# Last layer's adapter of a Trainium2 kernel: masked over all eight adapters, or gathered for each sequence onto strips of the array

## The chip, the cores and the metric

The kernel runs on one core of one Trainium2 chip. The metric is the device time of one execution in microseconds. A trace of one execution, taken by the hardware profiler, comes with it: it lists the instructions of TensorE (PE, with its weight loads as PEld), VectorE (DVE), ScalarE (ACT), GpSimd (POOL) and SyncE (SP), the DMA transfers, and the waits between them.

## The reference

Four layers are added in turn to x, which holds 64 sequences of 64 tokens with 512 features, in fp32. The first multiplies each sequence by a matrix chosen for it, the second is a linear layer with a low-rank adapter, the third attends over a paged cache in a window of 256 positions. The fourth is the one that is changed:

```python
# x: (64, 64, 512); W: (512, 512); A: (8, 16, 512); Bm: (8, 512, 16); adapter_idx: (64,)
H = jnp.einsum('btd,od->bto', x, W)
A_b = A[adapter_idx]
B_b = Bm[adapter_idx]
s_b = scalings[adapter_idx]
xa = jnp.einsum('btd,brd->btr', x, A_b)
delta = jnp.einsum('btr,bor->bto', xa, B_b)
x = x + H + delta * s_b[:, None, None]
```

In the third layer a sequence has eight query heads, four key heads and a block table; the keys and values that its window can reach are gathered by index. The index of the adapter lies in 0 to 6, one for each of the 64 sequences.

## The kernel before

There are two stages. The first (until about 450 us of the trace) goes through 32 tiles of 128 tokens, two sequences each: it runs the first two layers, the queries, keys and values of the third, the writing of new cache rows, and all index arithmetic. Its order is written out by hand in a loop over n, and small pieces of setup are hung onto single values of n. One of these is `adapters` (L425 to L441): for the last layer it builds `mask3`, with a row for each of the 128 pairs of adapter and rank and a column for each sequence; an entry is the adapter's scaling where the sequence uses that adapter, and otherwise zero. Another is `late_inputs` (L388): its last part loads the adapter's two matrices, `a3_sb` and `bm_sb`, whole.

The second stage goes through 16 groups q of four sequences. A group has eight steps, one for each sequence b and each pair of key heads gp; the step within a group is i, from 0 to 7. A step s does, in this order on TensorE:

- `scores(s + 1)` (psc, L975): the two key heads of the next step, each on 64 rows of the array;
- `turn_p(s)` (pp, L1017): six transposes of this step's softmax weights;
- in steps 4 to 7 a `k_turn` (psk, L175): four transposes of the next group's keys;
- one entry of the list `parts`, described below;
- `values(s)` (po, L1033): weights times values, each of two key heads on 64 columns of the array;
- in steps 3 to 6 another `k_turn`.

VectorE and ScalarE do the softmax of step s + 1 meanwhile (`maxima`, `exponentials`, `shares`), copy the transposed weights (pT, L1024) and the transposed keys (`kT_mem`, L183 and L184), and ScalarE and VectorE make the window's penalty `pen` (L963 to L965) in every second step. po needs both copies pT of its step.

GpSimd issues the gathers of the cache, all in the helper at L65, in program order: `v_load` (four for each sequence, into `vs_mem`, three sequences ahead), `v_patch` (one, into `vt_mem`, after ScalarE's `v_copy` at L197), and for each group `k_patch` in step 1 and `k_load` in steps 2 and 3, for keys of a later group. `v_share` (L208) then moves 28 rows of the values inside SBUF over SyncE's queue. In group 0, and only there, TensorE, VectorE and GpSimd also finish the last queries (`product_q`, L258; `norm_q`, where GpSimd has L232, L233 and L244; `turn_q`, L272).

`parts` is filled at the end of a group by `last_parts(q)` and worked off in the eight steps of the next, one entry in each. Entries 0 to 3 are `out_product` (pso, L1051): the attention's output product for 128 features, added to `xq` by VectorE (L1054). Entries 4 to 7 are the last layer: in step 4 the ranks (psxa, L1059) of all eight adapters for 256 tokens, their product with the mask on VectorE (xa, L1062), and half of the base product of the first 128 tokens (psy, L1070); in step 5 its other half (L1076), the product of the masked ranks with `bm_sb` (L1078), ScalarE's copy `ys` (L1081) and the store; in steps 6 and 7 the same for the other 128 tokens. `residual3` (L672) has added the identity to the transposed W beforehand, so that psy holds the residual too. After group 15 the list of eight parts runs alone, one after another.

PSUM tiles pso, psxa and psy come from one pool of two banks, `psM`.

Of the kernel before, what the change touches and what calls it, by code (L numbers as in the profile page):

```python
# [10 lines left out]
F32 = mybir.dt.float32  # L11
I32 = mybir.dt.int32
# [38 lines left out]
def kernel(  # L51
# [58 lines left out]
    w3_sb = ctile([P, KC, D], F32, "w3_sb")  # L110
    a3_sb = ctile([P, KC, P], F32, "a3_sb")
    bm_sb = ctile([P, D], F32, "bm_sb")
    iod = ctile([P, 3, 4, 28], F32, "iod")
    ion = ctile([P, 3, 4, 28], F32, "ion")
    mask3 = ctile([P, B], F32, "mask3")
    cen = ctile([P, B], F32, "cen")
# [166 lines left out]
    with ExitStack() as one:  # L283
# [104 lines left out]
        def late_inputs(part):  # L388
            h = slice(part % 2 * 2, part % 2 * 2 + 2)
            if part < 2:  # L390
                S.dma_start(out=woT_sb[:, h], in_=woT[:, h])
            elif part < 4:
                S.dma_start(out=w3_sb[:, h], in_=w3T.rearrange("(c p) o -> p c o", p=P)[:, h])
            else:
                S.dma_start(out=a3_sb, in_=a3T.rearrange("(c p) r -> p c r", p=P))
                S.dma_start(out=bm_sb, in_=bm3)

# [14 lines left out]
        def rows0():  # L412
# [9 lines left out]
            for h, hs in halves():  # L422
                V.tensor_scalar(
                    cidx[hs], condf[hs].rearrange("p (n two) -> p n two", two=2)[:, :, h],
                    float(T), tcol[hs], ALU.mult, ALU.add)  # L425

        def adapters(ad_i, scb, e, dst):
# [442 lines left out]
        for n in range(NLAST):  # L870
# [40 lines left out]
            if n % 4 == 3:  # L911
                mixers(n // 4 + 2)
            if 5 <= n < 10:
                late_inputs(n - 5)
            if 14 <= n < 18:
                positions(n - 14)
            if n == 19:
                adapters(ad3_i, sc3b, 8, mask3)
                middles()
# [123 lines left out]
    def last_parts(q):  # L1043
# [12 lines left out]
        def ranks():  # L1056
            ps = bank(psM, f"psxa{q}")
            for c in range(KC):
                PE.matmul(ps[:, :256], lhsT=a3_sb[:, c, :], rhs=xq[:, c],  # L1059
                          start=(c == 0), stop=(c == KC - 1))  # L1060
            xa[0] = mp.tile([P, 4, T], F32, name=f"xa{q}", tag="xa")
            V.tensor_tensor(  # L1062
                xa[0], ps[:, :256].rearrange("p (b t) -> p b t", t=T),
                mask3[:, 4 * q : 4 * q + 4].unsqueeze(2).to_broadcast([P, 4, T]), ALU.mult)

        def y_first(i):
            n = 2 * q + i
            psy[i] = bank(psM, f"psy{n}")
            for c in range(2):
                PE.matmul(psy[i], lhsT=xq[:, c, i * P : (i + 1) * P], rhs=w3_sb[:, c, :],  # L1070
                          start=(c == 0), stop=False)

        def y_rest(i):
            n = 2 * q + i
            for c in range(2, KC):
                PE.matmul(psy[i], lhsT=xq[:, c, i * P : (i + 1) * P], rhs=w3_sb[:, c, :],  # L1076
                          start=False, stop=False)
            PE.matmul(psy[i], lhsT=xa[0].rearrange("p b t -> p (b t)")[:, i * P : (i + 1) * P],  # L1078
                      rhs=bm_sb, start=False, stop=True)
            ys = ap2.tile([P, D], F32, name=f"ys{n}", tag="ys")  # L1080
            S.copy(ys, psy[i])  # L1081
            S.dma_start(out=out[n * P : (n + 1) * P, :], in_=ys)

        return [lambda ec=ec: out_product(ec) for ec in range(KC)] + [
            lambda: (ranks(), y_first(0)), lambda: y_rest(0), lambda: y_first(1), lambda: y_rest(1)]

# [22 lines left out]
    for s, (q, b, gp) in enumerate(steps):  # L1109
# [13 lines left out]
        if i in (2, 3):  # L1123
            k_load(q + 2, i - 2)
        scores(s + 1)
        turn_p(s)
# [82 lines left out]
```

## Time and profile before

| | |
|---|---|
| time, median of 3 runs (lowest, highest) | 1235.95 us (1233.83, 1238.47) |
| profiled execution: its own time | 1233.95 us |
| profiled execution: span of the trace | 1232.2 us |
| mean granted TensorE clock | 0.976 |
| second stage, from the first po to the end | 491.3 to 1232.2 us |
| one group, po to po eight steps later, groups 2 to 14 | mean 44.6 us |
| psxa in a group: 8 records, start to start | 1.76 us |
| one gather of `vs_mem` on GpSimd, mean | 1206 ns |

A row of the trace that begins with L names the line of the kernel, the engine, the operation, the tile that is written and, after the arrow, what is read; then the shape and the count; in brackets the idle time of the engine before it and what ended it. A matmul of fp32 operands appears as two records. A matmul's recorded duration includes its way through the array, so consecutive records overlap, and a rate is read from the distance of their starts. For TensorE a shape such as 124*64 gives the rows and columns of the array that are used.

### The profile page before, as it was taken

What the parts mean: (1) busy time and instruction counts of PE and PEld (TensorE: products, weight loads), DVE (VectorE), ACT (ScalarE), POOL (GpSimd) and SP (SyncE); (2) the same over time, 40 slices, a digit from 0 to 9 for tenths busy, and PEclk for the clock granted to TensorE, in tenths of its full rate; (3) what the DMA queues carried; (4) which work ended last, traced back from release to release, by engine and by line L of the source; (5) the groups of instructions that cost most, each with busy time, mean ns of one, the idle gap of its engine ahead of it and who ended that gap; (6) DMA issues with size and microseconds to landing.
All of it is one profiled execution on the core that took longest, in us unless ns stands there. A gap on an engine that the chain in (4) does not pass through costs nothing.

```text
span 1232.2 us, 17756 instructions
## 1 busy us (share of the span) xinstructions
PE 1112.6 (90%) x5622; PEld 642.5 (52%) x5622; DVE 750.7 (61%) x2312; ACT 568.2 (46%) x1471; POOL 613.4 (50%) x603
## 2 busy tenths in 40 slices
PE   4999899999999968788998998899999999999998
PEld 4444434444444434455655665555665565655565
DVE  3785347767656656784665664665665665666561
ACT  1332222233222435454665664665665665566651
POOL 3243322332335346776556655656666665665520
PEclk9999999999999988898999998999999999999999
DMA  8375613223342493636455645645745654665420
GB/s 265 126 265 212 227 39 112 96 78 106 98 141 67 148 182 96 162 88 151 130 133 132 157 116 112 149 119 133 167 127 131 152 142 110 154 145 132 98 63 35
DMA packets 129820, 163.20 MB, mean 132 GB/s; under 512 B 58079, under 2 KB 96891, under 8 KB 125545
## 3 DMA queue, kind: packets, MB, share of 16 engines
q0 software_dynamic: 63872, 85.04, 28.9%
q1 hardware_dynamic: 55632, 62.28, 16.8%
q10 hardware_dynamic: 10224, 14.76, 3.5%
q8 instruction: 45, 0.74, 0.3%
q14 instruction: 47, 0.39, 0.1%
HBM read 139.66 MB, written 50.33 MB: 154 GB/s over the span
## 4 chain that ended last, share of the span: by engine, by line
PE 73%; DVE 8%; DMA 6%; issue 5%; POOL 4%; ACT 3%; another core or an unknown queue 0%; ACTq 0%; SPq 0%; POOLq 0%; DVEq 0%
PE pso L1051 8%; PE pp L1017 8%; PE ps L776 7%; PE po L1033 7%; PE kv L809 7%; PE psc L975 7%; PE q L258 5%; PE psy L1076 5%; PE psy L1070 4%; PE psk L175 4%; PE psxa L1059 2%; PE ps L778 2%; PE psy L1078 2%; PE ps L752 2%; POOL vs_mem L65 2%
## 5 line engine op out<-in xcount | busy, mean ns | idle before, releaser
L65 POOL DMA_INDIRECT vs_mem<-in_vblk_dram,iv_old x256 | 308.9, 1206 | 78.1 <-issue 72.2
L65 POOL DMA_INDIRECT vt_mem<-pv,iv_new x64 | 81.1, 1266 | 177.3 <-ACT vt_mem L197 99.1
L1001 ACT ACTIVATE sm_mem<-sm_mem,mn 128x336 f32<-128x336 f32 x256 | 145.6, 574 | 38.1 <-DVE mn L991 31.9
L991 DVE CUSTOM_DVE_ANT_0 sm_mem<-psc,pen 128x336 f32<-128x336 f32 x256 | 119.8, 500 | 49.9 <-PE pp L1017 23.0
L1033 PE MATMUL po<-pT,vt_mem 124*64 124x128 f32 x1536 | 118.8, 282 | 14.4 <-issue 7.5
L1033 PEld LDWEIGHTS po<-pT,vt_mem 124*64 124x64 f32 x1536 | 84.7, 136 | 89.7 <-ACT sm_mem L1001 45.6
L258 PE MATMUL q<-wq_sb,x2q 128*128 128x512 f32 x256 | 120.0, 614 | 6.9 <-DMA x2q<-x2d 6.9
L1017 PE MATMUL pp<-ident,sm_mem 128*124 128x128 f32 x768 | 117.5, 287 | 7.5 <-DVE rsum L1008 3.3
L1051 PE MATMUL pso<-oT,woT_sb 128*128 128x256 f32 x512 | 122.3, 383 | 0.8 <-ACT oT L1041 0.8
L1017 PEld LDWEIGHTS pp<-ident,sm_mem 128*124 128x124 f32 x768 | 82.9, 141 | 73.0 <-issue 63.2
L975 PE MATMUL psc<-kT_mem,qs 64*128 64x336 f32 x512 | 110.0, 507 | 10.7 <-DVE kT_mem L184 10.1
L809 PE MATMUL kv<-wkv_sb,xr 128*128 128x512 f32 x256 | 117.1, 602 | 1.1 <-DVE k L224 1.1
L776 PE MATMUL ps<-kT_mem,kT_mem 128*128 128x512 f32 x256 | 117.0, 600 | 0.6 <-PE ps_fill L482 0.6
L1009 DVE TENSOR_SCALAR sm_mem<-sm_mem,rsum 128x336 f32<-128x336 f32 x256 | 105.3, 411 | 9.1
L1051 PEld LDWEIGHTS pso<-oT,woT_sb 128*128 128x128 f32 x512 | 91.8, 191 | 13.5 <-ACT pen L965 1.9
L244 POOL TENSOR_TENSOR q<-q,rsq 128x512 f32<-128x512 f32 x30 | 32.2, 1073 | 128.9 <-DVE rsq L242 82.4
L175 PE MATMUL psk<-ident,k 84*128 84x84 f32 x512 | 64.9, 254 | 34.8 <-ACT kT_mem L184 9.1
L258 PEld LDWEIGHTS q<-wq_sb,x2q 128*128 128x128 f32 x256 | 49.8, 199 | 65.7 <-issue 56.3
L1024 DVE COPY pT<-pp 124x384 f32<-124x384 f32 x128 | 70.8, 553 | 21.6 <-PE pp L1017 7.9
L776 PEld LDWEIGHTS ps<-kT_mem,kT_mem 128*128 128x128 f32 x256 | 49.0, 192 | 61.6 <-issue 60.7
L809 PEld LDWEIGHTS kv<-wkv_sb,xr 128*128 128x128 f32 x256 | 47.5, 193 | 58.4 <-issue 55.6
L1024 ACT COPY pT<-pp 124x384 f32<-124x384 f32 x128 | 61.8, 482 | 33.5 <-PE pp L1017 30.1
(223 smaller groups left out, 1750.4 us busy)
## 6 DMA issues: line engine op xcount, KB each, us to landing
xt<-in_x_dram SPq DMA_DIRECT2D x32, 256.0 KB
x2d<-xr SPq DMA_DIRECT2D x8, 1024.0 KB
x2q<-x2d SPq DMA_DIRECT2D x32, 256.0 KB
qd<-qt SPq DMA_DIRECT2D x64, 128.0 KB
qs<-qd SPq DMA_DIRECT2D x16, 512.0 KB
xq<-x2d SPq DMA_DIRECT2D x16, 512.0 KB
out_dram<-ys ACTq DMA_DIRECT2D x32, 256.0 KB
vt_mem<-vt_mem SPq DMA_DIRECT2D x192, 28.0 KB
```

The lines of the kernel that those rows point to most:

```text
L65: G.indirect_dma_start(out=dst, out_offset=None, in_=src, in_offset=bass.IndirectOffsetOnAxis(ap=idx, axis=0), **more,)
L175: PE.transpose(ps[:, oq, :], k2[:NP, 4 * oq + o4, 2 * gp : 2 * gp + 2].rearrange("p g d -> p (g d)"), ident[:NP, :NP])
L258: PE.matmul(psq[n], lhsT=xt[:, c, :], rhs=wq_sb[:, c, :], start=(c == 0), stop=(c == KC - 1))
L776: PE.matmul(ps, lhsT=wb_sb[:, c, oc * P : (oc + 1) * P], rhs=x1_mem[:, c, :], start=(c == 0), stop=False)
L809: PE.matmul(pskv[n], lhsT=xrs[s][:, c, i * P : (i + 1) * P], rhs=wkv_sb[:, c, :], start=(c == 0), stop=(c == KC - 1))
L975: PE.matmul(pscs[s][g], lhsT=qts[q][gs, gp, b % 4].rearrange("p h t -> p (h t)"), rhs=kT(q, gp)[gs, b % 4].rearrange("p o c i -> p (o c i) ...
L991: V.tensor_tensor_reduce(rows4(sm)[:, :, :, :28], rows4(pscs[s][g]), rows4(pens[b]), SCALE, 3.0e38, ALU.add, ALU.min, mn)
L1001: S.activation(w, w, AF.Exp, bias=mn, scale=-1.0, accum_out=rsum)
L1017: PE.transpose(pp[:NVK, o, :], sms[s][g][0][:, o * P : o * P + NVK], ident)
L1024: (V.tensor_copy if g else S.copy)(pT, pps[s][g][:NVK])
L1033: PE.matmul(po[g * HD : (g + 1) * HD, :], lhsT=vt(b)[:NVK, o, 2 * gp + g], rhs=pTs[s][g][:, o, :], start=(o == 0), stop=(o == 2))
L1051: PE.matmul(o, lhsT=woT_sb[:, c, ec * P : (ec + 1) * P], rhs=oT[:, c // 2, :, c % 2, :], start=(c == 0), stop=(c == 3))
```

## The change

The last layer's adapter is no longer held for all eight adapters. For each group the weights of its four sequences are gathered by GpSimd: four gathers (`a_load`) of 128 rows of 256 bytes into `a3_mem`, one for each sequence, and one gather (`b_load`) of 128 rows of 2 KB into `b3_mem`. They are issued in steps 5, 6 and 7 of the group whose tokens they are for; the products that read them run in steps 4 and 5 of the next group.

The ranks of one tile of 128 tokens (two sequences, 16 ranks each) take 32 columns of the array. There are four strips of 32 columns: token tile i (0 or 1) and feature chunk c modulo 2 choose the strip, and chunks c and c + 2 add up in it. `b3_mem` holds the output rows twice for each token tile, so the product with the ranks also sums the two strips; that product takes 64 rows of the array for each token tile. The mask remains, now to keep, of the two sequences on a strip, the one that the token belongs to, with its scaling.

The base product's chunks are divided otherwise over the steps: in step 4 the first chunk of the first tile, in step 5 the first chunk of the second tile and both products with the ranks, in steps 6 and 7 three chunks and the store of one tile each.

In the first stage, `last_adapters` takes the place of the second call of `adapters`, at the same place in the order; it makes the two index lists `ia3` and `ib3` and the new mask. The fifth part of `late_inputs` goes.

```diff
-    a3_sb = ctile([P, KC, P], F32, "a3_sb")
-    bm_sb = ctile([P, D], F32, "bm_sb")
+    a3_mem = ctile([P, 4, 16, KC], F32, "a3_mem")
+    b3_mem = ctile([P, D], F32, "b3_mem")
-    mask3 = ctile([P, B], F32, "mask3")
+    mask3 = ctile([P, B // 4, 2], F32, "mask3")
+    ia3 = ctile([P, B], I32, "ia3")
+    ib3 = ctile([P, B // 4], I32, "ib3")
...
-            else:
-                S.dma_start(out=a3_sb, in_=a3T.rearrange("(c p) r -> p c r", p=P))
-                S.dma_start(out=bm_sb, in_=bm3)
...
+        def last_adapters():
+            adf = t1([P, B], F32, "adf8")
+            V.tensor_copy(adf, ad3_i)
+            V.tensor_scalar(ia3, adf, float(P), pcol, ALU.mult, ALU.add)
+            seq_i, r_i = t1([P, 1], I32, "seq_i"), t1([P, 1], I32, "r_i")
+            own_s, r_f = t1([P, 2], F32, "own_s"), t1([P, 1], F32, "r_f")
+            V.tensor_copy(seq_i, pcol)
+            V.tensor_scalar(r_i, seq_i, 15, None, ALU.bitwise_and)
+            V.tensor_copy(r_f, r_i)
+            V.tensor_scalar(seq_i, seq_i, 4, 1, ALU.arith_shift_right, ALU.bitwise_and)
+            V.tensor_copy(own_s[:, 1:], seq_i)
+            V.tensor_scalar(own_s[:, :1], own_s[:, 1:], -1.0, 1.0, ALU.mult, ALU.add)
+            scl, part = t1([P, B], F32, "scl8"), t1([P, B], F32, "part8")
+            V.tensor_scalar(scl, adf, 0.0, sc3b[:, :1], ALU.is_equal, ALU.mult)
+            for e in range(1, 8):
+                V.tensor_scalar(part, adf, float(e), sc3b[:, e : e + 1], ALU.is_equal, ALU.mult)
+                V.tensor_tensor(scl, scl, part, ALU.add)
+            pick = part[:, : B // 2].rearrange("p (q s) -> p q s", s=2)
+            for h, hs in halves():
+                own_b = own_s[hs].unsqueeze(1).to_broadcast([HD, B // 4, 2])
+                two = slice(2 * h, 2 * h + 2)
+                V.tensor_tensor(mask3[hs], scl[hs].rearrange("p (q i) -> p q i", i=4)[:, :, two],
+                                own_b, ALU.mult)
+                V.tensor_tensor(pick[hs], adf[hs].rearrange("p (q i) -> p q i", i=4)[:, :, two],
+                                own_b, ALU.mult)
+            idx = scl[:, : B // 4]
+            V.tensor_reduce(idx, pick, AX.X, ALU.add)
+            V.tensor_scalar(ib3, idx, 16.0, r_f, ALU.mult, ALU.add)
...
             if n == 19:
-                adapters(ad3_i, sc3b, 8, mask3)
+                last_adapters()
                 middles()
...
         def ranks():
-            ps = bank(psM, f"psxa{q}")
+            ps = bank(psM, f"psxa{q}")[:, :P]
             for c in range(KC):
-                PE.matmul(ps[:, :256], lhsT=a3_sb[:, c, :], rhs=xq[:, c],
-                          start=(c == 0), stop=(c == KC - 1))
+                for i in range(2):
+                    lo = i * 64 + c % 2 * 32
+                    PE.matmul(ps[lo : lo + 32, :],
+                              lhsT=a3_mem[:, 2 * i : 2 * i + 2, :, c].rearrange("p b r -> p (b r)"),
+                              rhs=xq[:, c, i * P : (i + 1) * P], start=(c < 2), stop=(c >= 2))
...
-        def y_first(i):
+        def y_base(i, cs, start=False, stop=False):
             n = 2 * q + i
-            psy[i] = bank(psM, f"psy{n}")
-            for c in range(2):
+            if start:
+                psy[i] = bank(psM, f"psy{n}")
+            for c in cs:
                 PE.matmul(psy[i], lhsT=xq[:, c, i * P : (i + 1) * P], rhs=w3_sb[:, c, :],
-                          start=(c == 0), stop=False)
+                          start=start and c == cs[0], stop=stop and c == cs[-1])
...
-            PE.matmul(psy[i], lhsT=xa[0].rearrange("p b t -> p (b t)")[:, i * P : (i + 1) * P],
-                      rhs=bm_sb, start=False, stop=True)
+        def y_ranks():
+            for i, hs in halves():
+                PE.matmul(psy[i], lhsT=xa[0][hs].rearrange("p b t -> p (b t)"), rhs=b3_mem[hs],
+                          start=False, stop=False)
...
-            lambda: (ranks(), y_first(0)), lambda: y_rest(0), lambda: y_first(1), lambda: y_rest(1)]
+            lambda: (ranks(), y_base(0, (0,), start=True)),
+            lambda: (y_base(1, (0,), start=True), y_ranks()),
+            lambda: (y_base(0, (1, 2, 3), stop=True), y_store(0)),
+            lambda: (y_base(1, (1, 2, 3), stop=True), y_store(1))]
+
+    def a_load(q, i):
+        gather(a3_mem[:, i].rearrange("p r c -> p (r c)"), a3T, ia3[:, 4 * q + i : 4 * q + i + 1])
+
+    def b_load(q):
+        gather(b3_mem, bm3, ib3[:, q : q + 1])
...
+        if i in (5, 6):
+            a_load(q, 2 * (i - 5))
+            a_load(q, 2 * (i - 5) + 1)
+        if i == 7:
+            b_load(q)
         scores(s + 1)
...
-        "a3T": a["L3_cond_A"].reshape(P, D).T,
+        "a3T": a["L3_cond_A"].reshape(8, 16, KC, P).transpose(0, 3, 1, 2).reshape(8 * P, 64),
```

More of the change, by code (lines that the diff above doesn't have):

```diff
@@ L912 @@
                 mixers(n // 4 + 2)
-            if 5 <= n < 10:
+            if 5 <= n < 9:
                 late_inputs(n - 5)
@@ L1056, in ranks, with y_store @@
         def ranks():
-            ps = bank(psM, f"psxa{q}")
+            ps = bank(psM, f"psxa{q}")[:, :P]
             for c in range(KC):
-                PE.matmul(ps[:, :256], lhsT=a3_sb[:, c, :], rhs=xq[:, c],
-                          start=(c == 0), stop=(c == KC - 1))
-            xa[0] = mp.tile([P, 4, T], F32, name=f"xa{q}", tag="xa")
+                for i in range(2):
[3 more added lines that the diff above has]
+                              rhs=xq[:, c, i * P : (i + 1) * P], start=(c < 2), stop=(c >= 2))
+            xa[0] = mp.tile([P, 2, T], F32, name=f"xa{q}", tag="xa")
             V.tensor_tensor(
-                xa[0], ps[:, :256].rearrange("p (b t) -> p b t", t=T),
-                mask3[:, 4 * q : 4 * q + 4].unsqueeze(2).to_broadcast([P, 4, T]), ALU.mult)
-        def y_first(i):
+                xa[0], ps.rearrange("p (b t) -> p b t", t=T),
+                mask3[:, q].unsqueeze(2).to_broadcast([P, 2, T]), ALU.mult)
+        def y_base(i, cs, start=False, stop=False):
             n = 2 * q + i
-            psy[i] = bank(psM, f"psy{n}")
-            for c in range(2):
+            if start:
+                psy[i] = bank(psM, f"psy{n}")
+            for c in cs:
                 PE.matmul(psy[i], lhsT=xq[:, c, i * P : (i + 1) * P], rhs=w3_sb[:, c, :],
-                          start=(c == 0), stop=False)
-        def y_rest(i):
-            n = 2 * q + i
[L1075 to L1078, printed above, removed]
-                      rhs=bm_sb, start=False, stop=True)
+                          start=start and c == cs[0], stop=stop and c == cs[-1])
[3 more added lines that the diff above has]
+                          start=False, stop=False)
+        def y_store(i):
+            n = 2 * q + i
             ys = ap2.tile([P, D], F32, name=f"ys{n}", tag="ys")
```

## The prediction

> **What bounds the kernel now.** I read the page first: busy shares, then the chain that ended last.
>
> ```profile
> PE 1112.6 (90%) x5622; PEld 642.5 (52%) x5622; DVE 750.7 (61%) x2312; ACT 568.2 (46%) x1471; POOL 613.4 (50%) x603
> PE 73%; DVE 8%; DMA 6%; issue 5%; POOL 4%; ACT 3%; another core or an unknown queue 0%; ACTq 0%; SPq 0%; POOLq 0%; DVEq 0%
> ```
>
> TensorE is the bound over most of the span, so matmul time taken out should shorten it, unless what remains waits for something else. That is a question of single steps, so next the timeline of TensorE through one group of four sequences, from its fifth step (columns: start, us, engine, line, operation, tiles, shape, count, idle before).
>
> ```profile
> 887.33 0.51 PE L175 MATMUL psk<-ident,k 84*128 84x84 f32 x4 [0.78 <-PE pp L1017]
> 887.68 1.93 PE L1059 MATMUL psxa<-xq,a_sb 128*128 128x256 f32 x8
> 889.44 1.88 PE L1070 MATMUL psy<-w_sb,xq 128*128 128x512 f32 x4
> 891.25 0.88 PE L1033 MATMUL po<-pT,vt_mem 124*64 124x128 f32 x12
> 892.06 0.51 PE L175 MATMUL psk<-ident,k 84*128 84x84 f32 x4
> 892.50 0.83 PE L975 MATMUL psc<-kT_mem,qs 64*128 64x336 f32 x4
> 893.27 0.87 PE L1017 MATMUL pp<-ident,sm_mem 128*124 128x128 f32 x6
> 893.98 0.46 PE L175 MATMUL psk<-ident,k 84*128 84x84 f32 x4
> 894.27 1.92 PE L1076 MATMUL psy<-w_sb,xq 128*128 128x512 f32 x4
> 896.03 1.02 PE L1078 MATMUL psy<-bm_sb,xa 128*128 128x512 f32 x2
> 896.98 0.88 PE L1033 MATMUL po<-pT,vt_mem 124*64 124x128 f32 x12
> ```
>
> An fp32 matmul is two records. Start to start, a full-array record costs 0.216 us at 256 columns (psxa, 1.76 / 8), 0.429 at 512 (psy) and 0.109 at 128. The po row is the key: twelve 128-column records on half the array's columns take 0.81 us where twelve in a row would take 1.31. Six slots of 0.109 are 0.65, so pairs run together, and 0.16 is lost on entering and leaving the tiling. Row halves do the same in psc: two slots of 0.28 (336 columns) are 0.56, 0.77 is taken, 0.21 is lost.
>
> GpSimd, which gets new work, I read in its own timeline.
>
> ```profile
> 893.75 1.25 POOL L65 DMA_INDIRECT vt_mem<-pv,iv_new  x1 [2.83 <-DMA vt_mem<-vt_mem]
> 905.00 1.24 POOL L65 DMA_INDIRECT vt_mem<-pv,iv_new  x1 [3.98 <-ACT vt_mem L197]
> 915.69 1.25 POOL L65 DMA_INDIRECT vt_mem<-pv,iv_new  x1 [3.38 <-PE pp L1017]
> ```
>
> Each line is a patch (`v_patch`) that must wait for ScalarE's `v_copy`; the number in brackets is GpSimd's idle time, of which 0.30 is the ordinary gap between gathers. Beyond the gaps it comes to about 9.8 us of a 43.9 us group (871.77 to 915.69); the other 34.1 us are 23 gathers of about 1.5 us, gap included.
>
> **What the Trainium skill says.** "TensorEngine Tiling (Array Packing)", Key Properties: changing the tiling mode drains TensorE, and tiles run independently. The trace agrees: the two losses above. "TensorE: Matmul & The Clock Gate", Part 3, measured 2.38x for three 32-column strips; no run here shows strips of 32, only the pairs. "SBUF — State Buffer", Door 1, says that a read crossing to a new 16-byte line at every access pays a penalty; the new adapter weights are read with a step of 4 fp32, just that, and nothing in this trace shows such a weight load.
>
> **The change part by part.**
>
> *Ranks (step 4 of a group).* Out: eight records of 256 columns, 1.73 us. In: sixteen of 128 columns on four strips: four slots of 0.109 = 0.44, plus two changes of tiling at some 0.15, 0.30, plus 0.02 of stagger: 0.76. That is 1.0 less. Bounds: below, nothing beyond 1.0; above, if the sixteen strided weight loads do not hide, each at the 0.072 us at which psk's 128-column loads follow one another, 1.15 + 0.30, and the saving is 0.3. I take 1.0, since loads of 64 columns hide fully in po.
>
> *Rank rows (step 5).* Out: four records of 512, 1.72 us. In: two row halves side by side, two slots of 0.429 + the 0.21 of psc = 1.07. Saving 0.65. Bounds 0 (no overlap) to 0.86.
>
> *The base products move between steps.* Records of psy with w3 per step 4/5/6/7: before 4/4/4/4, afterwards 2/2/6/6; the two bm products before were in 5 and 7. What each step gives:
> - Step 4 loses 1.0 + 0.86 = 1.86 of TensorE. But po then waits for the pT copies of ScalarE and VectorE, which come late there: ScalarE stands behind the window's `pen` and the psk copy. Setting, in 13 groups, the new po to the later of TensorE and the last pT copy gives 0.6 to 3.3, median 1.3, mean 1.7 (three with a low clock give most). I take 1.6.
> - Step 5: 2.57 becomes 0.86 + 1.07 + 0.05; the VectorE copy of pT ends 5.1 us after the last po, against 5.72 now, so 0.6 comes through.
> - Step 6 gains two records, +0.86. TensorE stands idle there for 0.45 before psk (900.32), as ScalarE's `pen` chain starts late behind the copy `ys`. That copy now comes a step later, and the idle time goes: +0.4.
> - Step 7: six records before and after, 0.
>
> Sum 1.8 per group.
>
> *The five gathers* go to GpSimd: two after `v_patch` of step 5, two after `v_load` of step 6, one after `v_patch` of step 7. Their semaphore waits (ranks of step 4, rank rows of step 5, the gather eight back) are met by then. Price: 128-row gathers (`wg`) take 0.98, the 92-row `vs_mem` 1.21; with the gap 1.3 to 1.5; I take 1.4. Four are 5.6 against 3.68 of slack (3.98 less the gap), itself 0.2 shorter because steps 5 and 6 together shrink by that: `v_patch` of step 7 is 2.1 late. With the fifth, 1.4 more against 3.08: `v_patch` and `k_patch` of the next step 1 are 0.4 late. Queued behind are four `v_load` gathers, due two steps later, and `k_patch`, whose rows psk needs in step 3. Against psk's start in 12 groups its landing has no room in two, 0.7 us in three, 1.9 to 6.8 in the others; the waits view has three waits of psk on it, 4.4 us in all. 0.4 us costs 0.1 a group; the 0.4 MB of new traffic ahead of it I put at 0.15 more. Bounds 0 to 1.2.
>
> So 1.55 per group, 15 groups: **-23.3**. The last part list runs alone after the loop: ranks -1.0, rank rows -0.65, but its last strips wait some 0.35 for VectorE's `xq`: **-1.3**.
>
> *Setup.* The new index and mask arithmetic stands where six VectorE instructions stood, on the chain:
>
> ```profile
> 297.14 0.19 DVE adf L431
> ...
> 298.15 0.06 DVE mask L441
> ...
> 298.38 0.19 DVE cen L625
> ```
>
> Those took 1.24. The new 29: fourteen alternate on one buffer, each waiting for the last, at about 0.235 (the bd products just before: 0.22 to 0.25), 3.3; fifteen small ones at 0.19, 2.85. Together 6.15, **+4.9**. TensorE already waits 0.72 at 303.3 behind this very chain, so all of it arrives. Bounds 2.5 to 5.5. The two loads taken off ScalarE's queue cost nothing now: it is two tenths busy there.
>
> *The first group.* There GpSimd also normalizes queries and is itself the chain:
>
> ```profile
> 548.17 1.25 POOL vs_mem L65
> ...
> 550.00 1.68 POOL rsq L233
> ...
> 552.92 0.33 PE pst L272
> ```
>
> Two of the new gathers stand ahead of that `rsq`: **+2.6** (bounds 0 to 5; the two before fall into 3.9 us of idle time).
>
> Sum: -23.3 - 1.3 + 4.9 + 2.6 = -17.1. The profiled execution took 1233.95 (span 1232.2), so 1216.9 on its scale; the median shown is 2.0 higher: **1219**.
>
> **Rivals.**
> 1. *Strips gain little* (weight loads show, or four don't overlap): 0.7 less a group, +10.5, about 1229. For it: the 16-byte step. Against: po's loads hide.
> 2. *Hidden anyway.* Step 4's stall is not TensorE's: gaps of 0.5 to 3.8 us before psk there come with the heaviest gathers, and what psxa gives up is waited for instead. Left is 0.6 - 0.4 - 0.25, so nothing in the loop, -1.3 in the tail and +7.5: about 1242. With a third of step 4's gain kept, 1234. Against: in most groups pT is ready over a microsecond before po.
> 3. *Slower: GpSimd becomes the bound.* Lateness at `k_patch` is five gathers less 6.6 us. At 2.0 us a gather (gap included) it is 3.4, and the 12 groups' room turns that into 1.6 a group: the whole gain is gone and setup remains, 1240. That is the point from which it decides; at 2.3 its work, 34.1 + 11.5, exceeds the group's 43.9, and 15 x 1.7 + 7.5 make 1267. Against: in the steady groups no gather takes over 1.34 plus the gap.
> 4. *The change does not do what it says*: the strips might be issued so that one strip's two records follow each other and nothing overlaps. Ranks then cost 1.75 + 0.3, 1.3 worse: about 1238. The pairs of po speak against it; it is counted with rival 1.
>
> **How the numbers follow.** Forecast 0.62, rivals 1 and 4 0.14, rival 2 0.11, rival 3 0.13. Half a per cent, 6.2 us, is about what a measurement of this kernel can tell from no change. Rival 1 lies at the edge of faster, so: faster 0.71, same 0.15, slower 0.14. The range: the forecast's best (step 4 at its full 1.86, no cost at `k_patch`, setup 2.5) is near 1206; upwards it takes in rivals 1, 4 and most of 2: 1206 to 1240.
>
> **What would show it.** Right: psxa with sixteen records in about 0.75 us; the two b3 products starting together, 1.07 to the next po; steps 5, 6, 7 near 5.1, 5.9, 6.5 us; GpSimd's slack before `v_patch` gone at step 7 and still there at step 5; 6 us of VectorE at 297. Wrong: psxa's weight loads one after another; psk waiting for the `k` DMA in most groups; a GpSimd without idle time. If a group's length (43.9 here, 44.6 on average) does not fall by over a microsecond, the forecast has failed.

## The result and the profile after

The changed kernel takes 1286.88 us (median of four runs, 1283.6 to 1290.58) beside 1235.78 for the kernel before: a ratio of 1.0403, 95% interval 1.0358 to 1.0449. It is slower, by 51 us, where 17 us of gain were forecast. The profiled execution took 1283.9 us, its span is 1282.1.

The page of the kernel after, busy TensorE and the chain that ended last:

```profile
PE 1114.2 (87%) x5750; PEld 632.2 (49%) x5750; DVE 757.2 (59%) x2334; ACT 568.5 (44%) x1471; POOL 697.6 (54%) x682
PE 59%; DMA 12%; DVE 9%; issue 8%; POOL 7%; ACT 3%; another core or an unknown queue 1%; SPq 0%; ACTq 0%; POOLq 0%; DVEq 0%
```

TensorE's share of the chain falls from 73% to 59%; DMA's doubles. GpSimd is busy for 84 us more. TensorE in steps 4 to 7 of a calm group (timeline, same columns as before):

```profile
917.38 0.68 PE L1092 MATMUL psxa<-xq,a_mem 128*32 128x128 f32 x16
917.99 1.12 PE L1105 MATMUL psy<-w_sb,xq 128*128 128x512 f32 x2
919.57 0.88 PE L1064 MATMUL po<-pT,vt_mem 124*64 124x128 f32 x12 [0.46 <-ACT pT L1055]
...
922.70 1.06 PE L1105 MATMUL psy<-w_sb,xq 128*128 128x512 f32 x2
923.69 1.13 PE L1111 MATMUL psy<-b_mem,xa 64*128 64x512 f32 x4
924.75 0.97 PE L1064 MATMUL po<-pT,vt_mem 124*64 124x128 f32 x12
```

The strips do what they should: sixteen records of psxa take 0.61 us from start to start (eight took 1.76 before), the two row halves 1.06. GpSimd in the same group, and in group 0 (its timelines):

```profile
922.23 1.24 POOL L65 DMA_INDIRECT vt_mem<-pv,iv_new  x1 [2.30 <-ACT vt_mem L199]
...
935.40 1.25 POOL L65 DMA_INDIRECT vt_mem<-pv,iv_new  x1 [0.30 <-issue]
...
947.00 1.24 POOL L65 DMA_INDIRECT vt_mem<-pv,iv_new  x1 [3.02 <-ACT k L159]
```

```profile
537.73 0.99 POOL L65 DMA_INDIRECT a_mem<-in_a3T_dram,ia  x1 [0.30 <-issue]
539.03 0.96 POOL L65 DMA_INDIRECT a_mem<-in_a3T_dram,ia  x1 [0.31 <-issue]
540.06 0.40 POOL L234 TENSOR_SCALAR rsq<-rsq 128x8 f32<-128x8 f32 x1
```

The patch of step 7 (935.40) has lost its idle time; in group 0 two gathers stand right ahead of `rsq`. The setup's chain on VectorE:

```profile
295.25 0.19 DVE L431 CAST adf<-ad_i 128x64 f32<-128x64 int32 x1
...
301.37 0.23 DVE L456 TENSOR_SCALAR ib<-scl,r_f 128x16 int32<-128x16 f32 x1
301.51 0.19 DVE L656 TENSOR_SCALAR cen<-kvbrf 128x64 f32<-128x64 f32 x1
```

It takes 6.26 us, 1.24 before. Stage by stage, in us (the second pair of traces is from E5 and E6 below; the first po stands at 476.9 us before and at 483.7 after, while the 491.3 in the table of the kernel before is the third po):

| part | forecast | before to after, first measurement | E5 to E6 |
|---|---|---|---|
| setup, to the first po | +4.9 | +6.8 | +7.3 |
| groups 0 and 1 | +1.0 | +7.5 | -12.5 |
| groups 2 to 14, each | -1.55 | +2.8 (44.6 to 47.4) | +2.0 (41.6 to 43.5) |
| these 13 groups | -20.2 | +36.6 | +25.7 |
| last seven steps | -1.6 | -0.1 | -1.6 |
| tail after the loop | -1.3 | -0.9 | -0.9 |
| span | -17.1 | +49.9 | +18.0 |

Groups 0 and 1 are no evidence: over all traces of this study group 0 takes 67.7 to 67.8 or 71.4 to 74.7 us and group 1 45.5 to 58.1, in either kernel. The 13 middle groups decide.

For the numbers that follow: the five sets of experiments ran on five different chips, and before took 1197 to 1200 us in four of them and 1233 in the other, near the first measurement, so each ratio is to before in its own set, and both levels are named where it matters.

### The profile page after: what moved, and what is told of

Same layout as the page of the kernel before. It is cut to its first block, busy times and chain, and to the rows that moved or that the text cites. A ratio compares the mean times of both kernels' runs of the same rounds, so it can differ in the third digit from the quotient of the medians.

```text
span 1282.1 us, 18145 instructions
## 1 busy us (share of the span) xinstructions
PE 1114.2 (87%) x5750; PEld 632.2 (49%) x5750; DVE 757.2 (59%) x2334; ACT 568.5 (44%) x1471; POOL 697.6 (54%) x682
## 4 chain that ended last, share of the span: by engine, by line
PE 59%; DMA 12%; DVE 9%; issue 8%; POOL 7%; ACT 3%; another core or an unknown queue 1%; SPq 0%; ACTq 0%; POOLq 0%; DVEq 0%
PE psy L1105 8%; PE pp L1048 7%; PE pso L1082 6%; PE po L1064 6%; PE psc L1006 5%; PE kv L840 5%; PE ps L807 5%; PE q L260 4%; PE psk L177 4%; POOL vs_mem L65 3%; DMA k<-pk,ik_new 2%; DMA pv<-vt_mem,zidx 2%; PE ps L809 2%; PE ps L783 2%; PE psy L1111 1%
## 5 line engine op out<-in xcount | busy, mean ns | idle before, releaser
L65 POOL DMA_INDIRECT vs_mem<-in_vblk_dram,iv_old x256 | 313.2, 1223 | 77.4 <-issue 72.8
L1032 ACT ACTIVATE sm_mem<-sm_mem,mn 128x336 f32<-128x336 f32 x256 | 145.7, 574 | 49.9 <-DVE mn L1022 40.1
L1064 PE MATMUL po<-pT,vt_mem 124*64 124x128 f32 x1536 | 124.4, 286 | 36.1 <-issue 16.3
L1064 PEld LDWEIGHTS po<-pT,vt_mem 124*64 124x64 f32 x1536 | 88.6, 138 | 116.3 <-issue 43.6
L1006 PE MATMUL psc<-kT_mem,qs 64*128 64x336 f32 x512 | 113.9, 523 | 28.5 <-issue 13.6
L1105 PE MATMUL psy<-w_sb,xq 128*128 128x512 f32 x256 | 132.6, 644 | 0.0
L1048 PE MATMUL pp<-ident,sm_mem 128*124 128x128 f32 x768 | 123.3, 296 | 8.5 <-DVE rsum L1039 5.0
L1048 PEld LDWEIGHTS pp<-ident,sm_mem 128*124 128x124 f32 x768 | 86.7, 146 | 77.8 <-issue 57.9
L1040 DVE TENSOR_SCALAR sm_mem<-sm_mem,rsum 128x336 f32<-128x336 f32 x256 | 108.2, 423 | 9.1
L1082 PEld LDWEIGHTS pso<-oT,woT_sb 128*128 128x128 f32 x512 | 91.8, 191 | 17.1 <-ACT oT L1072 4.2
L177 PE MATMUL psk<-ident,k 84*128 84x84 f32 x512 | 67.6, 261 | 36.1 <-ACT kT_mem L186 6.6
```

The source lines that it names most:

```text
L65: G.indirect_dma_start(out=dst, out_offset=None, in_=src, in_offset=bass.IndirectOffsetOnAxis(ap=idx, axis=0), **more,)
L1006: PE.matmul(pscs[s][g], lhsT=qts[q][gs, gp, b % 4].rearrange("p h t -> p (h t)"), rhs=kT(q, gp)[gs, b % 4].rearrange("p o c i -> p (o c i) ...
L1032: S.activation(w, w, AF.Exp, bias=mn, scale=-1.0, accum_out=rsum)
L1048: PE.transpose(pp[:NVK, o, :], sms[s][g][0][:, o * P : o * P + NVK], ident)
L1064: PE.matmul(po[g * HD : (g + 1) * HD, :], lhsT=vt(b)[:NVK, o, 2 * gp + g], rhs=pTs[s][g][:, o, :], start=(o == 0), stop=(o == 2))
L1082: PE.matmul(o, lhsT=woT_sb[:, c, ec * P : (ec + 1) * P], rhs=oT[:, c // 2, :, c % 2, :], start=(c == 0), stop=(c == 3))
```

## The experiments

Two numbers are worked out for each trace, over groups 2 to 14: the length of a group, and GpSimd's work in it (its gathers' records, plus the 0.30 us gap after each; the memsets of E15 and E18 are counted without a gap). The two waits are from TensorE's waits, in us over the whole run.

| run | ratio to before (95%) | group | GpSimd's work | psk waits for the `k` DMA | po waits for the `vt_mem` DMA |
|---|---|---|---|---|---|
| E5 before | (1) | 41.6 | 34.0 | 6.6 | 4.1 |
| E6 after | 1.0107 (1.0019 to 1.0196) | 43.5 | 41.0 | 35.6 | 6.5 |
| E1 before, with the gathers | 1.0104 (1.0039 to 1.017) | 43.7 | 40.5 | 21.3 | 3.6 |
| E2 after, no gathers | 0.9816 (0.9772 to 0.986) | 39.7 | 34.4 | 7.0 | 3.2 |
| E3 after, plain loads | 0.9816 (0.9768 to 0.9864) | 40.2 | 34.2 | 8.2 | 6.5 |
| E17 the same again | 0.9796 (0.9762 to 0.9831) | 39.4 | 34.2 | 3.9 | 4.0 |
| E18 plain loads, busy GpSimd | 1.0135 (1.0098 to 1.0173) | 42.3 | 41.3 | 13.8 | 3.9 |
| E4 after, setup spread | 1.011 (1.0072 to 1.0148) | 43.2 | 41.0 | 35.6 | 6.0 |
| E7 `k_patch` first | 1.0524 (1.0451 to 1.0597) | 46.0 | 40.4 | 3.2 | 51.0 |
| E8 early gathers, `k_patch` first | 1.0501 (1.0422 to 1.0581) | 45.9 | 40.5 | 2.6 | 48.5 |
| E9 early gathers | 1.0175 (1.0096 to 1.0254) | 43.8 | 40.9 | 5.2 | 41.9 |
| E10 after, `q_load` in step 5 | 1.0061 (1.0031 to 1.0091) | 43.1 | 41.1 | 19.0 | 10.9 |
| E11 early gathers, `q_load` in step 5 | 1.0056 (1.0026 to 1.0085) | 42.6 | 41.1 | 11.6 | 20.3 |
| E12 before, `q_load` in step 5 | 0.9979 (0.9953 to 1.0004) | 41.7 | 34.1 | 6.1 | 0.5 |
| *beside a before of 1233:* | | | | | |
| E13 two gathers | 0.9966 (0.9934 to 0.9998) | 44.0 | 36.7 | none listed | 0.7 |
| E14 two gathers, `q_load` in step 5 | 0.9957 (0.9932 to 0.9981) | 44.6 | 36.7 | 1.0 | none listed |
| E15 plain loads, busy GpSimd | 1.0076 (1.0039 to 1.0113) | 45.1 | 41.1 | 3.4 | 1.8 |
| E16 five gathers, balanced | 1.0273 (1.0218 to 1.0328) | 47.1 | 40.6 | 0.3 | 2.3 |

The waits of E13 to E16 can't be set beside the others. A wait is told from records of semaphore updates, and of the 16 landings of a `k_patch` these four traces, like the two of the first measurement, hold only 3 to 12; the other traces hold 12 or more. TensorE's idle time ahead of psk in groups 2 to 14, whatever ended it, doesn't depend on such records: 12.5 us in E5 and 34.2 in E6, but 22.2 in before and 21.0 in after of the first measurement, and 14.0, 22.3, 25.6 and 24.3 in E13 to E16.

### E1 to E3: gathers or TensorE?

E1 puts five gathers of the same sizes into the kernel before, into spare tiles; E2 takes them out of the kernel after from group 1 on, so that the later groups use the first group's adapters; E3 fetches as many bytes over SP, from fixed rows.

```diff
 # E1, in the kernel before
+        if i in (5, 6):
+            a_load(q, 2 * (i - 5))
+            a_load(q, 2 * (i - 5) + 1)
+        if i == 7:
+            b_load(q)
 # E2, in the kernel after (and likewise for i == 7)
-        if i in (5, 6):
+        if q == 0 and i in (5, 6):
 # E3, in the kernel after
-        gather(b3_mem, bm3, ib3[:, q : q + 1])
+        DMA.dma_start(out=b3_mem, in_=bm3)
```

> The kernel before, with the five gathers of the change at the places the change gives them (two behind v_patch of step 5, two behind v_load of step 6, one behind v_patch of step 7), same rows and bytes, into tiles that nothing reads; all products, masks and loads of before stay. Theory G (the gathers themselves delay the other engines): the change lost 2.8 us a group net of 1.45 us saved in step 4, so the gathers alone cost about 4.2 us a group; with group 0 and 1, 1236 + 16 x 4 = about 1295 us, granted clock about 0.95, the excess in steps 5 to 7 and the next 0 and 1. Theory T (the regrouped TensorE work is what costs): at most the 0.25 us a group that I had forecast for the patches, 1236 to 1243 us, clock 0.97.

> The kernel after, with the adapter gathers issued in the first group of four sequences only, so that the later groups multiply by the first group's adapters. Theory G: the TensorE side of the forecast is left, about -1.5 us a group, and +6.8 us in the setup, so 1236 - 15 x 1.5 - 1 + 7 = about 1220 us, clock 0.975, steps 5 to 7 no longer than before. Theory T: near the kernel after, 1275 to 1285 us.

> The kernel after, with the same bytes fetched at the same places by plain DMAs on SP's queue, without GpSimd (fixed rows, so every group multiplies by the same adapters). If the gathers cost by their bytes and small packets (256 bytes a row for the ranks), it stays near 1285 us. If they cost by GpSimd and its queue, it falls to about 1220 us, as without gathers.

Where before takes 1197 us, the gathers cost it, and neither their bytes nor the new TensorE work does: without them, or with as many bytes over SP, 1.8% is gained. E1 lost less than theory G's 4.2 us a group: 2.1 against E5. The telling pair is E1 and E6. They have five such gathers each, E6's TensorE steps are 2.2 us shorter where the gathers are left out (E2), and yet their groups are about equally long, 43.7 and 43.5, with ratios of 1.0104 and 1.0107. TensorE's saving is real (E2), and little of it is left while the gathers are there. How little is not sharp: E1's trace is of its slowest execution (1220.95 us, median 1213.09), and E6's ratio also bears the longer setup. By the medians E6's groups could be some 0.4 us shorter (an estimate: 6 us over 15 groups, within the intervals).

### E4: the setup

The 29 instructions of `last_adapters` were cut into four parts.

```diff
-                last_adapters()
...
+            if n in (24, 26, 28, 30):
+                last_adapters((n - 24) // 2)
```

> The kernel after, with the 29 VectorE instructions of last_adapters taken from stage 19 of the setup and issued in four parts in stages 24, 26, 28 and 30. If all of the setup's 6.8 us is this chain and the low clock that follows TensorE's wait for it, the first po comes 6 to 7 us earlier and the time is about 1280 us; if only the five extra microseconds of VectorE count, 1282 us; if the setup's loss comes from elsewhere (the end of the setup waits on a DMA), 1286 us.

The first po comes at 480.8 us, beside 486.0 and 484.3 in E2 and E3 of the same set. Over all traces it comes at 475.6 with the setup of before (four traces), 483.3 with the chain in one piece (nine) and 479.1 with the chain spread (seven), so spreading regains about 4 of 7.7 us on average; single traces of one kind scatter over 3 to 9, and the time doesn't show it (1.011, beside E6's 1.0107 in another set).

### E5 and E6: before and after under the same conditions

> The kernel before, unchanged, for a trace under the same conditions as the other experiments (their comparison runs of before took 1197 us, against 1236 in the first measurement). If k_patch (the patch of the key rows, fetched in step 1, needed by psk in step 3) is on its edge already here, psk waits for it some 0 to 1 us a group, its landing comes 9 to 10 us after its issue, and the interval from the po of step 3 to that of step 4 is 7.1 us or a little more; with about 1197 us in all a group takes about 42 us.

> The kernel after, unchanged, beside the same runs of before as the next two. Theory K (k_patch lands late, because it is issued later and because the software queue still has the b3 rows and the v_load behind them to move): as the run with the setup spread, some 6 us slower: ratio 1.015; the excess over the run without gathers sits in step 4's interval, 2.5 to 3.5 us a group, and steps 5 to 7 are not longer. Theory L (all engines release late while the gathers run): 1.04 as in the first measurement, with the excess in steps 5 to 7.

Theory K's picture: the loss sits in step 4's interval (from the po of step 3 to that of step 4), 7.27 to 8.73 us on average, and in step 3's, 4.11 to 4.77; steps 5 to 7 are near the forecast. Here is the same place in both traces. First before (E5): GpSimd's and SP's timelines and TensorE's, around the po of step 1 at 854.19.

```profile
842.51 1.25 POOL L65 DMA_INDIRECT vt_mem<-pv,iv_new  x1 [4.69 <-ACT vt_mem L197]
...
854.09 1.02 POOL L65 DMA_INDIRECT k<-pk,ik_new  x1 [0.30 <-issue]
```

```profile
851.89 0.54 SPq L953 DMA_DIRECT2D qs<-qd  x1
```

```profile
864.06 0.51 PE L175 MATMUL psk<-ident,k 84*128 84x84 f32 x4 [0.79 <-DMA k<-pk,ik_new]
```

Then after (E6), po of step 1 at 860.10:

```profile
850.13 1.25 POOL L65 DMA_INDIRECT vt_mem<-pv,iv_new  x1 [0.30 <-issue]
...
860.53 1.01 POOL L65 DMA_INDIRECT k<-pk,ik_new  x1 [0.30 <-ACT sm_mem L1032]
```

```profile
859.08 1.88 SPq L984 DMA_DIRECT2D qs<-qd  x1
```

```profile
872.83 0.82 PE L177 MATMUL psk<-ident,k 84*128 84x84 f32 x4 [3.64 <-DMA k<-pk,ik_new]
```

Counted from the po of step 1, the patch of step 7 goes from -11.7 to -10.0 us, `q_load` (qs) from -2.3 to -1.0, `k_patch` from -0.1 to +0.4, and psk from 9.9 to 12.7. `q_load` moves because SP issues it behind `v_share`, which waits for that patch (from 540 to 1150 us of the trace `v_share` waits 346 us for patches to land in E5, and 354 in E6). From its issue to its landing `k_patch` takes 9.3 us in E5 and 11.3 in E6 (mean of twelve groups); in that time 1.17 MB on the software queue and 0.14 MB on the others start to move in E5, 1.48 and 0.59 in E6: `q_load`'s 512 KB and part of a late `v_load` have come into its flight. And before has no room there: its nine waits of psk for this DMA say so.

The waits are not the whole price. After a wait like this TensorE runs at half its clock for a while: the psk above takes 0.82 us instead of 0.51. In groups 2 to 14 the half clock lasts 44.4 us in E6, 3.4 in E2 and nothing in E5. From E2 to E6, TensorE's idle time grows by 2.5 us a group, and the half clock costs up to 1.6 more (an estimate: half of the 41.0 us that are new, over 13 groups). Together that is 4.1, and the group grows by 3.8.

### E7 to E12: other orders

E7 issues `k_patch` ahead of `v_patch` in step 1. E8 also has two buffers for the rank weights, their gathers in steps 4 and 5, `b_load` in step 6, and the spread setup. E9 is E8 without E7's move, E10 is after with `q_load` moved, E11 is E9 with `q_load` moved, and E12 is before with `q_load` moved.

```diff
 # E7
             v_share(b + 1)
+            if i == 1:
+                k_patch(q + 1)
             v_patch(b + 2)
-        if i == 1:
-            k_patch(q + 1)
 # E8, E9, E11
-        if i in (5, 6):
-            a_load(q, 2 * (i - 5))
-            a_load(q, 2 * (i - 5) + 1)
-        if i == 7:
+        if i in (4, 5):
+            a_load(q, 2 * (i - 4))
+            a_load(q, 2 * (i - 4) + 1)
+        if i == 6:
             b_load(q)
 # E10 to E12
-        if i == 2:
+        if i == 5:
             q_load(q + 1)
```

> The kernel after with one change: in step 1, GpSimd issues k_patch ahead of v_patch instead of behind it, so it no longer waits for ScalarE's v_copy and a gather of 1.25 us. Theory K: k_patch is issued up to 3 us earlier and lands 9 to 11 us after that; psk's wait for it falls from 35 us to under 10, and the time falls by about 13 x 2 = 26 us, to a ratio near 0.995. Theory L, or a bound by GpSimd's total work: within 5 us of the kernel after.

> The kernel after with the rank weights in two buffers, so that their gathers can stand in steps 4 and 5 (two behind v_load, two behind v_patch) and that of the b3 rows in step 6; with k_patch ahead of v_patch in step 1; and with the setup's arithmetic spread over stages 24 to 30. Theory K: everything is off k_patch's way; a group as without gathers, 39.7 us, and setup of 480 us: about 1172 us where before takes 1197, ratio 0.98. If gathers cost by slowing TensorE's releases wherever they stand: no better than the setup spread alone, 1.01.

> As the run with early gathers and k_patch first, but k_patch again behind v_patch. Theory Q (the five gathers make v_patch of step 7 late; v_share, and behind it on SP's queue q_load, then start 2 us later, so that q_load's 512 KB and part of a v_load move while k_patch is under way and delay its landing by 2 us): with the rank weights fetched in steps 4 and 5 and the b3 rows in step 6 nothing is late at step 7, k_patch lands about 9.2 us after its issue again, a group takes 39.7 to 40.5 us, and with the shorter setup the ratio to before is about 0.98. Theory P (the gathers cost by the work they add to the software queue, wherever they stand): a group of 43 us or more, ratio 1.005 to 1.05.

> The kernel after with one change: q_load (512 KB on SP's queue) stands in step 5 instead of step 2. Theory Q: 0.44 of the 0.75 MB that are new in k_patch's window go, so its landing comes 1.3 us sooner (about 10 us after issue, still issued 0.5 us late), psk's wait falls from 35 to some 15 us, and the time falls by 15 to 20 us, to a ratio of about 0.995. Theory P: q_load is on another queue and changes nothing, ratio 1.01.

> Early gathers, spread setup, k_patch behind v_patch, and q_load in step 5. Theory Q: as without q_load moved or a little better, since q_load can't fall into k_patch's window in any group: 39.5 us a group, ratio 0.97 to 0.98. Theory P: 1.005 or more.

> The kernel before with q_load in step 5 instead of step 2. There psk's waits for k_patch are 6.6 us in all and q_load's transfer ends mostly before k_patch is issued: a gain of 0 to 6 us, ratio 0.995 to 1.0.

Five of these six expectations fell in part or whole; E12's held. What theory P gives for E9 and E11 came out (43.8 us and 1.0175; 1.0056), and theory Q's figures there did not. E7 and E8 ended psk's wait, as theory K says, and put a larger one elsewhere; TensorE's waits of E6, then of E7:

```profile
PE psk L177 <- DMA k<-pk,ik_new: 35.6, 14, 4.6
```

```profile
PE po L1064 <- DMA vt_mem<-vt_mem: 51.0, 25, 7.0
```

With `k_patch` ahead, `v_patch` is issued and lands late, `v_share` behind it, and po has no values. In E9, meant to have nothing late at step 7, that patch is issued 5.2 us after the po of step 6 (2.6 in before, 5.3 in E6): the rank gathers ran into steps that had no idle time to give. Theory Q holds for `q_load` as far as psk's wait goes: moving it took that from 35.6 to 19.0 us and the flight from 11.3 to 9.3 us (E10). It is not the whole: a group fell by 0.4 us only, the time from 1.0107 to 1.0061 with intervals that overlap, and no order of five gathers brought a group below 42.6 us.

### E13 to E18: is it GpSimd's time?

The column with GpSimd's work suggests why. In E5 a group gives it 34.0 us of work in 41.6. Without the gathers the group shrinks to 39.7 and the work does not: of the idle time ahead of the patches, gap taken off, 5.2 us are left (E2) of 7.5 (E5). The five gathers are 6.6 us, more than that. That is theory R. E13 and E14 need two gathers for a group, since the rank weights are fetched as rows of 2 KB by the list of the b3 rows and turned by TensorE. E16 keeps five, each behind a `v_load`, where GpSimd would wait. E15 and E18 are the plain loads of E3 with a memset of GpSimd at each place.

```diff
 # E13 (in E14 b_load is in step 7, q_load in step 5)
+        def a_turn():
+            ps = bank(psM, f"psat{q}")
+            for c in range(KC):
+                PE.transpose(ps[:, c * P : (c + 1) * P], an_mem[:, c * P : (c + 1) * P], ident)
+            V.tensor_copy(at_mem.rearrange("p c r -> p (c r)"), ps)
...
+        gather(an_mem, a3T, ib3[:, q : q + 1])
...
+        if i == 6:
+            a_load(q)
             b_load(q)
 # E15 and E18, in a_load and b_load of E3
+        G.memset(idle_mem, 0.0)
 # E16
+        if i == 0 and q:
+            a_load(q - 1, 2)
+            a_load(q - 1, 3)
+        if i == 4:
+            a_load(q, 0)
+        if i == 6:
+            a_load(q, 1)
             b_load(q)
```

> The kernel after with two gathers a group instead of five: the rank weights as 128 rows of 2 KB by the same index list as the b3 rows, turned by four transposes on TensorE in step 2 (0.44 us, and one VectorE copy of 0.6 us) instead of gathered in turned form; both gathers behind v_load of step 6, and the setup spread. Theory R (GpSimd's own time is the bound: without the new gathers it has 4.5 us to spare in a group of 39.2 us, and five gathers of 1.28 us take 6.4): two take 2.6, which fits; a group of 39.7 to 40.5 us, setup as before plus 6 us at most, 1170 to 1180 us, ratio 0.975 to 0.985. Theory Q (what is late at step 7 pushes q_load into k_patch's way): the same. Theory P (any work on the software queue costs): 1.0 or more.

> As the run with two gathers, with the b3 rows in step 7 behind v_patch instead of step 6, and q_load in step 5. Theory R: the same, within 0.5 per cent. Theory Q: v_patch of step 7 no longer late at all and q_load out of the way: a group of 39.3 to 39.7 us, up to 0.5 per cent better.

> The run with plain loads on SP's queue (0.98 of before), with a memset of 1.28 us on GpSimd at each of the five places, so that GpSimd spends the gathers' time without a gather. Theory R: GpSimd's time is what costs, so v_patch of step 7 is about 2 us late and k_patch 0.5, as with the gathers: near the kernel after, ratio 1.0 to 1.01. If it is the gathers' packets on the software queue: as with the plain loads, 0.98 to 0.985.

> The kernel after with the setup spread and its five gathers placed behind v_load only, where GpSimd would wait for v_patch anyway: one in step 4, two (one of them the b3 rows) in step 6, two in step 0 of the next group. Theory Q (only lateness at v_patch of step 7 matters, and placement avoids it): a group of 40 us or less, ratio 0.98. Theory R (GpSimd has 4.5 us to spare and needs 6.4): the group can't be shorter than about 41.1 us plus what the waits between the queues add, ratio 0.995 to 1.01.

E16 speaks against theory Q as the whole cause: the patch of step 7 comes 2.9 us after the po of step 6, nearly as in before (2.6), and the kernel is still 2.7% slower. But it also misses theory R's 0.995 to 1.01, and so do E13 and E14 miss R's group of 39.7 to 40.5 us: theirs take 44.0 and 44.6, beside 44.6 in the first measurement's before. With 0.3% and 0.4% under before, at the edge of what the intervals tell, they are still the only kernels here with gathered adapters that are not slower than before. E15 had no run with plain loads beside it; E17 and E18 are that pair, in one set:

> The run with plain loads on SP's queue once more, to stand beside the next one on one chip (before took 1197 us beside it the first time, but 1233 us beside the run with the busy GpSimd). Theory R and the packet theory both expect it clearly below before: 0.98 to 0.99.

> The run with plain loads and five memsets of 1.28 us on GpSimd a group once more. Theory R (GpSimd's time): 1.5 to 3 per cent above the run with plain loads, with v_patch of step 7 and k_patch issued later. Packet theory: within 0.5 per cent of it. Half of that difference would mean that both count.

The same loads, without one more gather, go from 0.980 to 1.0135 when GpSimd is kept busy for 6.7 us a group (four memsets of 1.34 and one of 1.29), and psk waits for `k_patch` again, 13.8 us instead of 3.9. That is 3.5%, above R's 1.5 to 3, and far from the packet theory's half per cent. There is a flaw in it: VectorE is slower as well. Its instructions that scale `sm_mem`, in E17 and E18 (busy us, mean ns of one, idle before):

```profile
L1040 DVE TENSOR_SCALAR sm_mem<-sm_mem,rsum 128x336 f32<-128x336 f32 x256 | 115.9, 453 | 9.1
```

```profile
L1041 DVE TENSOR_SCALAR sm_mem<-sm_mem,rsum 128x336 f32<-128x336 f32 x256 | 160.8, 628 | 9.0
```

Of the 2.9 us that a group grows by, 0.9 are in step 4's interval, where psk waits; 1.4 are in step 6's, where I put them down to these slower instructions. So E18 shows that a busy GpSimd without more gathers brings psk's wait back, not how much of the loss it is. For the sets with a before of 1197 to 1200 us the weight of the case lies on E1 beside E6, and on about 41 us of work in groups of 42.6 to 43.8 (E1, E4, E6, E9 to E11): GpSimd is idle there, gaps aside, for only 1.5 to 3.2 us a group. In E7 and E8, whose groups take 46, it is idle for 5.5.

### What stays open

In the first measurement the loss was 4.0%, under the conditions of E6 1.1%. The rest looks different in the trace, and what was found so far doesn't explain it. TensorE's waits for `k_patch` in before and in after of the first measurement:

```profile
PE psk L175 <- DMA k<-pk,ik_new: 3.6, 2, 1.9
```

```profile
PE psk L177 <- DMA k<-pk,ik_new: 5.9, 5, 2.3
```

These two are undercounts, but TensorE's idle time ahead of psk didn't grow either (22.2 to 21.0 us in groups 2 to 14). Nor was GpSimd full: 6.6 us of a group of 47.4 were idle. What grew is the idle time ahead of po, 7.7 to 29.0 us, and ahead of psc, 8.8 to 22.1. All together it grew by 38.3 us or 2.9 a group; the half clock, 13.7 to 51.2 us there, adds up to 1.4 (an estimate as above). That makes 4.4, as much as the group lost against the forecast: it grew by 2.8 and was to shrink by 1.55. In these pauses TensorE, ScalarE and VectorE stand still together; timelines of TensorE and of ScalarE at one such place:

```profile
882.78 0.51 PE L177 MATMUL psk<-ident,k 84*128 84x84 f32 x4
887.09 1.49 PE L1006 MATMUL psc<-kT_mem,qs 64*128 64x336 f32 x4 [3.79 <-issue]
```

```profile
885.72 0.27 ACT L1072 COPY oT<-po 128x128 f32<-128x128 f32 x1 [2.21 <-remote]
```

po had ended at 882.86 by the trace and ScalarE had nothing to do, but its copy of po starts 2.9 us later; psc comes after 3.8 us of idle time, at half the clock (1.49 us for 0.83). Updates of TensorE's semaphore more than 0.7 us after the last modelled end before them: 87 in before and 133 in after of the first measurement, 2 in each of E5 and E6; 72 to 122 in E13 to E16, E15 with its plain loads among them. (The count is rough, since a tenth or more of these updates has no record in the traces with many late ones.) So the late releases, that is, the updates that other engines wait for, belong to the conditions under which before takes 1233 to 1236 us, not to the gathers alone. There the gathers cost more: after 1.040 and E16 1.027, but E15, as busy on GpSimd without them, 1.008. So there GpSimd's time alone doesn't account for the loss. What makes the releases late was not found, nor whether it goes with the chip or with the occasion.

## Why the prediction was wrong

*TensorE's part was right, where a run shows it alone.* In intervals from po to po, medians of E5 and E2: step 4 7.16 to 5.30 (-1.9, forecast -1.6), step 5 5.72 to 5.06 (-0.7, forecast -0.6), step 6 5.53 to 5.81 (+0.3, forecast +0.4), step 7 6.45 both (0). That is -2.2 before rounding, against -1.8; the mean group fell by 1.9. psxa took 0.61 us against 0.76, the row halves 1.06 against 1.07. The 16-byte step of the new weights shows in their loads (median 137 ns each in after, 110 in E13, which loads 32 columns without the step), but the loads hide. The tail gave -0.9 against -1.3.

*The step that failed is the cost of the five gathers, 0.25 us a group, bounds 0 to 1.2.* In E6 beside E2 they cost 3.8 (43.5 less 39.7). In the first measurement, where no run leaves them out, the groups are 4.4 us longer than forecast; E14, with two gathers, a spread setup and `q_load` moved, is 0.4% under a similar before where after is 4.0% over it. The price of a gather was about right: 0.98 to 1.03 us plus 0.30, against 1.4 in all. So was the lateness: `v_patch` of step 7 is 2.2 us late in the first measurement and 2.8 in E6, against 2.1; `k_patch` 0.2 and 1.1 on average, against 0.4. What was wrong is what that costs. For the 3.8 of E6 the runs show this much, while most of the loss in the first measurement stays open (see above):

- *The slack was read from a group that other waits had made long.* The forecast took 9.8 us of idle GpSimd in a group of 43.9. The same kernel has 7.5 in a group of 41.6, and the shorter group that the change aims at has 5.2. Work of 34.1 and 7.0 us against an aim of 42.3 was 97% of it, by the forecast's own numbers, and GpSimd also waits for others at given places: in E6 it is at work for 41.0 of 43.5 us.
- *`k_patch`'s room was taken from the same trace*, as 0.7 to 6.8 us in ten of twelve groups. In E5 there is next to none: psk waits for it nine times. The trace that the room was read from holds only 4 to 11 of each patch's 16 landings, so the last of them may have come later than it shows.
- *SP's queue was not followed.* The 2.1 us at step 7 were called absorbed. But `v_share` waits for that patch, `q_load` stands behind it, and its 512 KB then move during `k_patch`'s flight: two microseconds more, where the forecast had 0.15 for the new traffic. E10 measures that term: psk's wait falls by 16.6 us when `q_load` is out of the way, though little of it reaches the time.
- *The patches were read as waiting for ScalarE's `v_copy` alone.* Of the three lines shown for them only one names it; the others name `v_share`'s transfer and a TensorE instruction.
- *No wait was priced with the half clock behind it*, up to 1.6 us a group in E6.

*Setup.* The chain took 6.26 us (forecast 6.15), and the first po came 6.8 later, against 4.9. TensorE's wait behind the chain grew from 0.7 to 5.8 us, as forecast; the rest is put down to the clock, which the trace grants at half from 305.0 to 315.3 us, where before ran at the full one; no run measures the clock's part alone. "TensorE: Matmul & The Clock Gate" in the Trainium skill, Part 1, has half rate follow an idle window of about 3.4 us, and the half-clock stretches of these traces last whole multiples of 3.41 us, one to four, where the end of the run doesn't cut them. From the first po to the end they grew from 35 to 92 us in the first measurement.

*Group 0.* `rsq` came 2.5 us late behind two gathers, as forecast (2.6), but whether the group is longer for it can't be told from a group that takes 67.7 or 72 us in either kernel.

*The rivals.* Rival 3 named the mechanism that fits E6, GpSimd as the bound, and put its point at 2.0 us a gather; it came at 1.3, because the point was worked out from the same slack. Rivals 1 and 4 are refuted by psxa. Rival 2, that step 4's gain is waited for elsewhere, is what E6 shows, from another cause than it gave.

## What to carry to other kernels

Before an engine off the path is given new work, compare its whole work in a period with the period that the change aims at, not with the idle time of the present trace: that time shrinks with the gain, and part of it comes from waits that other conditions don't have. Follow each late instruction into every queue that waits for it, down to the large transfers behind, and see whose flight they fall into. Where such an engine is nearly full, moving its work mostly changed who waits here (E7 to E11); taking instructions away from it (E13 and E14, two wide gathers and a turn on TensorE for five narrow ones) gave the only gathered kernels that are not slower than before, by a hair and under the slower conditions alone. Before room is read from a trace, see whether its landing records are complete.

## What was not expected of the hardware

- A gather of 128 rows took GpSimd 0.98 us with rows of 2 KB and 1.03 with rows of 256 bytes (E6, means): GpSimd's time went with the count of gathers and not with their bytes.
- With memsets of 128 x 1400 on GpSimd (about 1.3 us each, five a group) VectorE's scaling of `sm_mem` took 628 ns on average instead of 453. "SBUF — State Buffer" in the Trainium skill says under its "single rule" that only the port pair which VectorE and GpSimd share makes engines wait for each other; E17 and E18 agree with such a wait.
- One kernel took 1197 us in some sets and 1233 in others, with releases coming late in the latter's traces (87 beside 2, by the rough count above) and with many landing records missing there.
